# Four buffers for fetched rows in place of eight, from quad 40 on, in a graph network layer

## The chip, the cores and the metric

The kernel runs on one core of a Trainium2 chip. The metric is the time of one execution in microseconds of device time; 1115.52 us is the median of three runs before the change. The core has five engines that run their own instruction streams in order and wait for each other by semaphores: TensorE (PE; its weight loads are listed as PEld), VectorE (DVE), ScalarE (ACT), GpSimd (POOL) and SyncE (SP). DMAs are issued from queues of SP and POOL.

## What is computed

A message-passing layer over 12,500 nodes of 128 features and 400,000 edges that are sorted by destination, with a residual and a layer norm. Cut to what matters:

```python
rbf = exp(-(distances[:, None] - centers) ** 2 / (2 * width * width))     # 50 centers
cut = 0.5 * (cos(pi * distances / 10) + 1) * (distances <= 10)
W = (silu(rbf @ fw1 + fb1) @ fw2 + fb2) * cut[:, None]
messages = (h[src] @ pw + pb) * W
agg = segment_sum(messages, dst, num_segments=12500)
out = layernorm(h + h + silu(agg @ mw1 + mb1) @ mw2 + mb2)
```

Edges longer than 10 contribute nothing, and most edges are longer.

## The kernel before

**Projection.** First all node rows are multiplied by `pw` and stored as a table `proj` in DRAM (lines 562 to 581), so that an edge needs one row of it.

**Packing.** The edges are taken in seven chunks. `pack(c)` (lines 352 to 557) is a generator of many small DVE steps that squeezes out the edges over the cut-off: each of 128 partitions shifts its survivors to the left; POOL then scatters them to a list in DRAM (`packed`, line 451); SP reads the list back (`pair`, line 467), DVE takes it apart (from line 476), PE turns source indices, places and cuts over the partitions, and DVE copies them to `srci`, `dl` and `cut`. Two chunks are in work at a time. Their steps are put between other DVE work by a planner.

**Quads.** What survives is worked on in 141 quads of 4 x 128 edges. For quad q:
- `fetch(q)` (line 593): four indirect DMAs on POOL's queue, 128 rows each, into one buffer `got` of a pool of eight. Quads 0 to 7 are fetched before the table is complete, as raw rows, and projected later (`multiply`).
- `radials`, `basis`, `first`, `tanh`, `silu`, `second`: lengths over SP's queue, ACT's Gaussians, PE, ACT and DVE make the filter `pu` of the quad in PSUM (two buffers).
- `message(q)` (line 671): DVE multiplies `pu` by `got`. It is the last reader of the buffer.
- `place(q)` (line 676): four DVE instructions make one-hot matrices `hot`, scaled by `cut`.
- `sum_up(q)` (line 689): PE multiplies `msg` by `hot`, into a bank shared by two quads.
- `add(q)` (line 712): two quads later DVE adds the result to `aggT` at an offset read from `base_i`.

From step 70 on, nodes whose edges are all in are finished between the quads (`nodes`, line 847); the rest follows the loop.

**The order.** It is written by hand: the loop over q at line 977 issues everything in program order, and each engine runs its part in that order. Within a step come: fetches, `second(q + 1)`, `message(q)`, `sum_up(q)`, `place(q + 1)`, `add(q - 2)`, pieces of packing. A planner with two clocks, `clock` for DVE and `pool` for POOL, decides only where fetches and pieces of packing stand. `fetches(until, most)` (line 343) issues fetches while POOL's clock is not past `until`, up to quad `most`; its cost is 5.15 us for a quad, not before the buffer is free by `summed`. Each step calls it twice, once up to `q + GOT` by the clock, once without regard to the clock up to `q + AHEAD`, which is q+3. At execution the planner's numbers play no part; there POOL runs as far ahead in its own stream as semaphores let it: a fetch waits for the last reader of its buffer, `message(q - 8)`, and for its DMA lane. POOL's stream holds besides the fetches the scatters of line 451 (one a chunk) and, at step 90 or so, the load of a counter `bad_i` (line 1028) that DVE computes after the last chunk.

Of the kernel before, what the change touches and what calls it, by code (L numbers as in the profile page):

```python
# [10 lines left out]
F32 = mybir.dt.float32  # L11
# [8 lines left out]
P = 128  # L20
# [5 lines left out]
QT = 4  # L26
# [12 lines left out]
NQ = QB[-1]  # L39
AHEAD = 3  # L40
AHEAD_X = 4
FROM_X = 8
GOT = 8


CLEARED = 3000
# [10 lines left out]
def kernel(  # L57
# [38 lines left out]
    N, H = x.shape  # L96
# [14 lines left out]
    work = ctx.enter_context(tc.tile_pool(name="work", bufs=2))  # L111
# [61 lines left out]
    def clear(pieces=1, to=N):  # L173

        while pieces and to_clear and to_clear[0][0] < to:
            a, b = to_clear.pop(0)
            nc.scalar.activation(aggT[:, a:b], iota_n[:, :b - a], AF.Copy, scale=0.0)
            pieces -= 1
# [155 lines left out]
    pool = [0.0]  # L334
    there_at = {}
    summed = {}
# [3 lines left out]
    most = [FROM_X]  # L340
    times = [0]

    def fetches(until, most):

        while fetched[0] < min(most, known[0]) and pool[0] <= until:
            q = fetched[0]
            fetch(q, table=x if q < FROM_X else None)
            pool[0] = max(pool[0], summed.get(q - GOT, 0.0)) + 5.15
            there_at[q] = pool[0] + 2.2
            fetched[0] += 1  # L350

# [239 lines left out]
    d_of, rbf_of, ph_of, t_of, s_of, pu_of, got_of, pa_of, hot_of = ({} for _ in range(9))  # L591

    def fetch(q, idx=None, table=None):
        got = work.tile([P, QT, H], F32, name="got", bufs=GOT)
        for j in range(QT):
            i = srci[:, 2 * q + j // 2, j % 2:j % 2 + 1] if idx is None else idx[:, j:j + 1]
            nc.gpsimd.indirect_dma_start(  # L597
                out=got[:, j, :], out_offset=None, in_=proj if table is None else table,
                in_offset=bass.IndirectOffsetOnAxis(ap=i, axis=0))
        got_of[q] = got  # L600
# [14 lines left out]
    def radials(to):  # L615

        while next_o[0] < min(to, -(-NQ // 2)):
            o = next_o[0]
            if not all(chunk_of(q) in stored for q in quads(o)):
                break  # L620
            radial(o, [near_d[2 * q:2 * q + 2].rearrange("(o p) e -> o (p e)", o=1)
                       for q in quads(o)])
            next_o[0] += 1

    def chunk_of(q):
        return max(c for c in range(NC_) if QB[c] <= q)

    def basis(o):
        d, n = d_of.pop(o)
        u = n * 64  # L630
        rbf = work.tile([P, QE], F32, name="rbf")
        nc.scalar.activation(rbf[:u], d[:u], AF.Square, bias=rbf_bias[:u], scale=rbf_scale[:u])  # L632
        nc.scalar.activation(rbf[:u], rbf[:u], AF.Exp, scale=-1.0 / (2.0 * width * width))  # L633
        rbf_of[o] = rbf, n

    def first(o):

        rbf, n = rbf_of.pop(o)
        ph = ps.tile([P, 2, QE], F32, name="ph", bufs=1)
        for h in range(n):  # L640
            p0 = h * 64
            nc.tensor.matmul(ph[:, h, :], w1_sb[p0:p0 + KR], rbf[p0:p0 + KR], start=True, stop=True)  # L642
        ph_of[o] = ph, n

    def tanh(o):
        ph, n = ph_of[o]
        t = work.tile([P, 2, QE], F32, name="t", bufs=1)
        nc.scalar.activation(t[:, :n], ph[:, :n], AF.Tanh, scale=0.5)  # L648
        t_of[o] = t
# [10 lines left out]
    def second(q):  # L660

        s = s_of.pop(q)
        pu = bank("pu")
        nc.tensor.matmul(pu, ones_b[:, :P], bias_b["fb2"].rearrange("k j f -> k (j f)"), start=True,  # L664
                         stop=False)
        for j in range(QT):
            nc.tensor.matmul(pu[:, j * H:(j + 1) * H], s[:, j * P:(j + 1) * P], fw2_h,  # L667
                             start=False, stop=(j == QT - 1))
        pu_of[q] = pu

    def message(q):
        msg = work.tile([P, QT, H], F32, name="msg")
        nc.vector.tensor_mul(msg, pu_of.pop(q).rearrange("p (j f) -> p j f", j=QT), got_of.pop(q))  # L673
        return msg
# [10 lines left out]
    def windows(q):  # L685

        return 1 if chunk_of(q) < WIDE_C else 2

    def sum_up(q, msg):
        hot = hot_of.pop(q)  # L690
        if q % 2 == 0:
            pa_of["two"] = bank("pa").rearrange("p (h n) -> p h n", h=2)
        pa = pa_of[q] = pa_of["two"][:, q % 2, :]
        n = QT // windows(q)
        for j in range(QT):
            k = j // n
            nc.tensor.matmul(pa[:, k * W:(k + 1) * W], msg[:, j, :], hot[:, j, :],  # L697
                             start=(j % n == 0), stop=(j % n == n - 1))
# [3 lines left out]
    def base_of(q, ks=(0, 1)):  # L702
        for k in ks:
            if k == windows(q):
                break
            _, v = nc.values_load_multi_w_load_instructions(
                base_i[0:1, 2 * q + k:2 * q + k + 1], engines=[mybir.EngineType.DVE],
                min_val=0, max_val=N - W,
                skip_runtime_bounds_check_because="bases are destinations, and at most N - W")
            bases[q, k] = v[0]  # L710
# [136 lines left out]
    def nodes(q):  # L847

        if ready:
            normalize(*ready.pop(0))  # L850
        for k, t0 in enumerate(early + last):
            if begin[t0] - 8 == q:
                load_x(t0)
            if begin[t0] + 3 == q and t0 in early:
                if k % 4 == 0:
                    st_of[0] = statistics()
                node_stats(t0, st_of[0][:, k % 4 * 4:])
                if k % 4 == 3 or k + 1 == len(early):
                    scaled(early[k // 4 * 4:k + 1], st_of[0])
            if begin[t0] + 2 == q and t0 in early:  # L860
                node_second(t0, "ms")
            if begin[t0] == q:
                node_first(t0)
            if begin[t0] + 1 == q:
                node_silu(t0)
        if q == NQ - 4:
            for t0 in range(0, NT, 4):
                if t0 not in begin:
                    load_x(t0)
# [26 lines left out]
    def go_on(c):  # L896
        v = next(chunks[c], None)
        if v is None:
            todo.remove(c)
        else:  # L900
            clock[0] += v
# [11 lines left out]
    def multiplies(until):  # L913
        while times[0] < min(FROM_X, fetched[0]) and there_at[times[0]] <= until:
            multiply(times[0])
            times[0] += 1
# [60 lines left out]
    for q in range(NQ):  # L977
        while todo and todo[0] <= chunk_of(min(q + 3, NQ - 1)):
            go_on(todo[0])
        nodes(q)  # L980
        most[0] = min(NQ, q + GOT)
        fetches(clock[0], most[0])
        fetches(math.inf, min(NQ, q + AHEAD + 1))
        assert fetched[0] > min(NQ - 1, q + AHEAD)
        multiplies(max(clock[0], there_at[min(q + 1, NQ - 1)]))
        if q >= CLEAR_Q:
            clear()
        if loads_later and q >= 8:
            nc.sync.dma_start(*loads_later.pop(0))
        radials(q // 2 + 5)  # L990
        if q % 2 == 0:
            if 2 * (q // 2 + 1) < NQ:
                tanh(q // 2 + 1)
        else:
            if q + 3 < NQ:
                first((q + 3) // 2)
            if q + 5 < NQ:
                basis((q + 5) // 2)
        if q + 1 < NQ:
            second(q + 1)  # L1000
        msg = message(q)
        sum_up(q, msg)
        if q > 1:
            base_of(q - 2, (0,))
        if q + 1 < NQ:
            place(q + 1)
        if q > 1:
            base_of(q - 2, (1,))
            add(q - 2)
        if q % 2 == 0 and 2 * (q // 2 + 1) < NQ:  # L1010
            silu(q // 2 + 1)
        clock[0] = max(clock[0], there_at[q])
        summed[q] = clock[0] + 0.7
        clock[0] += (1.9 if q % 2 else 3.1) + 0.3 * (windows(q) - 1)
        if q == 1:
            clear_packed(2, nc.sync)
        if q + 1 < NQ:
            pack_until(max(there_at[q + 1], clock[0] + PACK_US), NC_)
        if NODES - 8 <= q < NODES - 2:
            part_of(*(("mb1", mb1_f) if q < NODES - 5 else ("mb2", mb2_f)), (q - NODES + 8) % 3)  # L1020
        elif q == NODES - 2:
            late["mw2"] = mw2_h = keep.tile([H, H], F32, name="mw2_h")
            nc.vector.tensor_scalar(mw2_h, mw2_sb, 0.5, None, op0=OP.mult)
        if not todo and not counted:
            counted.append(q)
            count()
        elif counted and total is None:
            total = nc.values_load(bad_i[0:1, 0:1], min_val=0, max_val=2 * E)
# [86 lines left out]
```

## Time and profile before

| what | value |
|---|---|
| median of three runs | 1115.52 us (1115.3 to 1117.06) |
| the profiled execution | 1117.06 us, of which the span (first to last instruction) is 1115.3 us |
| mean granted TensorE clock | 0.752 |
| message(0), (36), (97), (140) start at | 122.7, 369.5, 828.5, 1086.3 us |
| fetch(40), (44), (140) start at | 346.7, 370.5, 1047.8 us |

Times within the span count from its first instruction. The four fetches of quad q are the (4q+1)th to (4q+4)th of the 564 instructions of line 597 on POOL, and message(q) is the (q+1)th of the 141 of line 673 on DVE; the timeline lists both. "Idle before" an instruction is time in which its engine had nothing running, with what ended it; "remote" there, and "another core or an unknown queue" in the chain of waits, mean that no releaser was found. Of the chain that ended last, this holds 17%:

```
DVE 24%; PE 22%; another core or an unknown queue 17%; issue 16%; POOL 13%; DMA 3%; ACT 2%; DVEq 2%; SPq 0%; POOLq 0%; ACTq 0%
```

### The profile page before, as it was taken

How to read it: one execution, taken by the hardware profiler on the slowest of the kernel's cores; microseconds unless marked ns; L12 is line 12 of the kernel's file. 1: busy time of each engine (PE TensorE's matmuls, PEld its weight loads, DVE VectorE, ACT ScalarE, POOL GpSimd, SP SyncE). 2: the span in 40 equal slices, each digit the busy share in tenths (PEclk: the TensorE clock that was granted, in tenths of full speed). 3: DMA queues.
4: the chain of work that ended last, by engine and by line, in shares of the span. 5: the costliest groups of instructions: out<-in, count | busy, mean ns of one | idle time of the engine just before them, and what ended most of it. 6: DMA issues, size and time to landing. Idle time of an engine off the chain costs nothing.

```text
span 1115.3 us, 11574 instructions
## 1 busy us (share of the span) xinstructions
PE 648.4 (58%) x3492; PEld 496.0 (44%) x3492; DVE 657.8 (59%) x1857; ACT 297.2 (27%) x473; POOL 560.5 (50%) x585
## 2 busy tenths in 40 slices
PE   6744757654572558526660674276377666666673
PEld 6734545443451446415440453155254554445462
DVE  7902469566583559637980786085364744655594
ACT  5423412113131233102320231042041422241132
POOL 1551366446637555657176416625556655666400
PEclk9867778667687668757785787588587786979796
DMA  7833422222123221313122112232143242142121
GB/s 222 248 100 105 139 72 62 63 69 85 53 71 87 59 57 55 99 40 105 51 82 62 49 46 67 64 107 62 43 121 87 65 126 69 55 125 79 36 61 44
DMA packets 88188, 91.85 MB, mean 82 GB/s; under 512 B 13864, under 2 KB 67832, under 8 KB 88120
## 3 DMA queue, kind: packets, MB, share of 16 engines
q1 hardware_dynamic: 69320, 52.77, 15.6%
q0 software_dynamic: 18544, 38.17, 12.5%
q8 instruction: 29, 0.48, 0.2%
q14 instruction: 39, 0.32, 0.1%
q10 hardware_dynamic: 256, 0.11, 0.0%
HBM read 75.29 MB, written 15.71 MB: 82 GB/s over the span
## 4 chain that ended last, share of the span: by engine, by line
DVE 24%; PE 22%; another core or an unknown queue 17%; issue 16%; POOL 13%; DMA 3%; ACT 2%; DVEq 2%; SPq 0%; POOLq 0%; ACTq 0%
POOL got L597 13%; DVE hot L681 6%; PE pu L667 5%; PE ph L642 5%; DVE s L655 4%; PE pa L697 4%; PE pa L275 2%; DVE msg L673 2%; DVE aggT L716 2%; DMA x<-in_x_dram 1%; PE pu L569 1%; PE pu L664 1%; DMA got<-proj,srci 1%; PE ms L728 1%
## 5 line engine op out<-in xcount | busy, mean ns | idle before, releaser
L597 POOL DMA_INDIRECT got<-proj,srci x532 | 516.6, 971 | 328.1 <-issue 145.3
L697 PE MATMUL pa<-hot,msg 128*128 128x128 f32 x1128 | 193.0, 325 | 194.2 <-DVE msg L673 174.3
L697 PEld LDWEIGHTS pa<-hot,msg 128*128 128x128 f32 x1128 | 173.5, 235 | 207.3 <-DVE msg L673 185.8
L681 DVE TENSOR_SCALAR hot<-iota_n,dl,cut 128x128 f32<-128x128 f32 x564 | 158.4, 352 | 133.9 <-remote 97.5
L673 DVE TENSOR_TENSOR msg<-pu,got 128x512 f32<-128x512 f32 x141 | 96.5, 685 | 183.8 <-remote 132.4
L667 PEld LDWEIGHTS pu<-fw_h,s 128*128 128x128 f32 x1128 | 185.8, 231 | 41.2 <-issue 33.8
L667 PE MATMUL pu<-fw_h,s 128*128 128x128 f32 x1128 | 187.6, 316 | 26.4 <-issue 26.0
L642 PE MATMUL ph<-rbf,w_sb 51*128 51x512 f32 x282 | 113.8, 884 | 145.2 <-DVE s L655 91.0
L648 ACT ACTIVATE t<-ph 128x1024 f32<-128x1024 f32 (+1 forms) x71 | 71.7, 1011 | 280.9 <-remote 151.9
L642 PEld LDWEIGHTS ph<-rbf,w_sb 51*128 51x128 f32 x282 | 29.8, 243 | 166.5 <-issue 124.7
L730 ACT ACTIVATE zt<-ms 128x512 f32<-128x512 f32 (+1 forms) x25 | 14.6, 587 | 324.6 <-remote 124.0
L655 DVE SCALAR_TENSOR_TENSOR s<-t,ph 128x1024 f32<-128x1024 f32 (+1 forms) x71 | 85.8, 1208 | 18.4 <-ACT t L648 12.4
L716 DVE TENSOR_TENSOR aggT<-aggT,pa 128x128 f32 x212 | 60.3, 284 | 13.6 <-remote 5.4
L664 PE MATMUL pu<-fb_b,ones_b 96*128 96x512 bf16 x141 | 64.0, 454 | 0.2 <-issue 0.2
L451 POOL DMA_INDIRECT packed<-line,at_i x7 | 6.9, 992 | 108.8 <-DVE line L447 51.2
L632 ACT ACTIVATE rbf<-d,rbf_bias,rbf_scale 128x512 f32<-128x512 f32 (+1 forms) x71 | 57.1, 804 | 6.8 <-DMA d<-near_d 6.7
L597 POOL DMA_INDIRECT got<-in_x_dram,srci x32 | 32.2, 1007 | 43.2 <-DVE part L519 33.1
L275 PEld LDWEIGHTS pa<-pw_sb,xT 128*128 128x128 f32 (+1 forms) x260 | 40.6, 226 | 27.6 <-ACT xT L571 15.7
L664 PEld LDWEIGHTS <-ones_b 96*128 96x128 bf16 x141 | 14.8, 105 | 82.9 <-issue 82.5
L275 PE MATMUL pa<-pw_sb,xT 128*128 128x128 f32 (+1 forms) x260 | 42.4, 315 | 15.3 <-ACT xT L571 13.0
L633 ACT ACTIVATE rbf<-rbf 128x512 f32<-128x512 f32 (+1 forms) x71 | 44.7, 630 | 2.2
L792 ACT ACTIVATE x<-x,by,rs 128x128 f32<-128x128 f32 x91 | 37.1, 482 | 8.8 <-DVE by L762 8.8
(172 smaller groups left out, 629.1 us busy)
## 6 DMA issues: line engine op xcount, KB each, us to landing
d<-near_d SPq DMA_DIRECT2D x141, 128.0 KB
x<-in_x_dram SPq DMA_DIRECT2D x48, 256.0 KB
got<-proj,srci POOLq DMA_INDIRECT x532
proj<-hp SPq DMA_DIRECT2D x24, 256.0 KB
out_dram<-x SPq DMA_DIRECT2D x24, 256.0 KB
packed<-zero_i SPq DMA_DIRECT2D x6, 188.0 KB
pair<-packed SPq DMA_DIRECT2D x3, 264.0 KB
r_d<-in_edge_weight_dram SPq DMA_DIRECT2D x3, 256.0 KB
```

The source lines that it names most:

```text
L275: nc.tensor.matmul(to[:m, k, :], lT[:, k * P:k * P + m], w, start=False, stop=(k == a + c - 1))
L597: nc.gpsimd.indirect_dma_start(out=got[:, j, :], out_offset=None, in_=proj if table is None else table, in_offset=bass.IndirectOffsetOnAxi ...
L632: nc.scalar.activation(rbf[:u], d[:u], AF.Square, bias=rbf_bias[:u], scale=rbf_scale[:u])
L642: nc.tensor.matmul(ph[:, h, :], w1_sb[p0:p0 + KR], rbf[p0:p0 + KR], start=True, stop=True)
L648: nc.scalar.activation(t[:, :n], ph[:, :n], AF.Tanh, scale=0.5)
L655: nc.vector.scalar_tensor_tensor(s[:, :n], t_of.pop(o)[:, :n], 1.0, ph[:, :n], op0=OP.add, op1=OP.mult)
L664: nc.tensor.matmul(pu, ones_b[:, :P], bias_b["fb2"].rearrange("k j f -> k (j f)"), start=True, stop=False)
L667: nc.tensor.matmul(pu[:, j * H:(j + 1) * H], s[:, j * P:(j + 1) * P], fw2_h, start=False, stop=(j == QT - 1))
L673: nc.vector.tensor_mul(msg, pu_of.pop(q).rearrange("p (j f) -> p j f", j=QT), got_of.pop(q))
L681: nc.vector.tensor_scalar(hot[:, j, :], iota_n[:, :W], dl[:, at[0], at[1]], cut[:, at[0], at[1]], op0=OP.is_equal, op1=OP.mult)
L697: nc.tensor.matmul(pa[:, k * W:(k + 1) * W], msg[:, j, :], hot[:, j, :], start=(j % n == 0), stop=(j % n == n - 1))
L716: nc.vector.tensor_add(to, to, pa[:, k * W:(k + 1) * W])
```

## The change

Fetched rows of quads 0 to 39 go to the eight buffers `got` as before. Those of quads 40 to 140 go to four other buffers, `got_later`. (A negative q, of a fallback branch that does not run with these inputs, goes there too.) The planner's terms follow: a quad of 44 or more is held to have its buffer when quad q-4 is summed, and the bound `most` is q+8 up to quad 44, then q+4.

```diff
+LATER = 40, 4
...
-            pool[0] = max(pool[0], summed.get(q - GOT, 0.0)) + 5.15
+            pool[0] = max(pool[0], summed.get(q - (GOT if q < sum(LATER) else LATER[1]), 0.0)) + 5.15
...
     def fetch(q, idx=None, table=None):
-        got = work.tile([P, QT, H], F32, name="got", bufs=GOT)
+        q_at = q if q >= 0 else NQ
+        got = (work.tile([P, QT, H], F32, name="got", bufs=GOT) if q_at < LATER[0] else
+               work.tile([P, QT, H], F32, name="got_later", bufs=LATER[1]))
...
-        most[0] = min(NQ, q + GOT)
+        most[0] = min(NQ, max(min(q + GOT, sum(LATER)), q + LATER[1]))
```

## The prediction

> **What bounds the kernel now.** I read the page first: its costliest groups, then the waits of the stretch in which the change acts, then the timeline of POOL and DVE, then a table of stretches.
>
> ```profile
> PE 648.4 (58%) x3492; PEld 496.0 (44%) x3492; DVE 657.8 (59%) x1857; ACT 297.2 (27%) x473; POOL 560.5 (50%) x585
> ...
> L597 POOL DMA_INDIRECT got<-proj,srci x532 | 516.6, 971 | 328.1 <-issue 145.3
> ...
> L673 DVE TENSOR_TENSOR msg<-pu,got 128x512 f32<-128x512 f32 x141 | 96.5, 685 | 183.8 <-remote 132.4
> ```
>
> No engine is busy for more than 59% of the span, so the time is in waits. One quad is four fetches on POOL; successive starts lie 1.25 us apart (971 ns each and 0.3 us between them), so a quad takes POOL 5.0 us. Message (line 673) stands behind 183.8 us of DVE's idle time, 132.4 of it with a releaser that the profile cannot name. The waits from 418 us (message of quad 44) to 828.5 us (quad 97), while chunks are still packed, for the most part:
>
> ```profile
> DVE msg L673 <- remote: 58.0, 7, 19.7
> ...
> POOL got L597 <- DVE msg L673: 55.7, 9, 22.3
> DVE hot L681 <- remote: 51.5, 6, 14.0
> POOL packed L451 <- DVE line L447: 51.2, 2, 28.3
> ```
>
> POOL waits for DVE here, and DVE waits for something unnamed. The timeline shows what lies beside the unnamed waits: first POOL, then DVE around 583 us.
>
> ```profile
> 451.97 0.98 POOL L451 DMA_INDIRECT packed<-line,at_i  x1 [14.48 <-DVE first L366]
> ...
> 555.45 0.98 POOL L451 DMA_INDIRECT packed<-line,at_i  x1 [22.88 <-DVE line L447]
> ...
> 673.25 0.98 POOL L451 DMA_INDIRECT packed<-line,at_i  x1 [28.29 <-DVE line L447]
> ...
> 762.47 0.97 POOL L597 DMA_INDIRECT got<-proj,srci  x1 [22.35 <-DVE msg L673]
> ```
> ```profile
> 582.78 0.83 PE L667 MATMUL pu<-fw_h,s 128*128 128x128 f32 x6
> ...
> 598.96 0.69 DVE L673 TENSOR_TENSOR msg<-pu,got 128x512 f32<-128x512 f32 x1 [17.41 <-remote]
> ...
> 613.67 1.12 DVE L681 TENSOR_SCALAR hot<-iota_n,dl,cut 128x128 f32<-128x128 f32 x4 [14.01 <-remote]
> ```
>
> The reader is to see a cycle. POOL runs ahead until its queue comes to an entry that needs DVE at a certain quad (the scatter of line 451, and at 762 us the load of bad_i, line 1028); it waits there for 14 to 28 us while DVE uses up the rows already fetched; then eight buffers are free and it issues fetches without a pause. From 555.4 to 608.6 us it issues 41 in a row. In this burst PE's last matmuls end at 583.6, but message starts only at 598.96; it waits for PE's semaphore, whose next recorded update is at 598.9. The update after it comes at 613.6, with the matmuls it reports over by 601.8. So while POOL issues for long, PE's completions arrive late, and DVE, ACT and then PE stand still. I don't know the cause; the coincidence holds for all DVE gaps of over 9 us after 418 us (14.0, 10.9, 17.4, 14.0, 19.7, 9.8, 16.1: 102 us), which lie in the four bursts of 28 to 41. By stretches (us, then PE, PEld, DVE, ACT and POOL busy with counts, granted clock, DMA share, GB/s):
>
> ```profile
> 467.60:498.40 30.80, 6.40 (x21) 4.25 (x21) 5.73 (x13) 0.00 (x0) 19.27 (x21) 0.50 0.16 46
> ...
> 577.00:617.60 40.60, 8.04 (x38) 6.29 (x39) 8.72 (x25) 2.84 (x4) 23.94 (x26) 0.58 0.25 71
> 617.60:684.30 66.70, 48.55 (x274) 35.70 (x270) 55.77 (x166) 16.73 (x22) 23.93 (x25) 0.86 0.20 57
> 684.30:728.90 44.60, 8.48 (x29) 6.03 (x29) 9.18 (x23) 8.46 (x17) 26.42 (x28) 0.50 0.20 58
> ...
> 828.50:1073.60 245.10, 165.44 (x892) 124.43 (x893) 145.26 (x430) 69.88 (x120) 136.47 (x144) 0.81 0.29 83
> ```
>
> **The change part by part.** It moves no instruction. Stepping through the planner's numbers (lines 343 to 350 and 981 to 984): its POOL clock stands later than its DVE clock from quad 33 on, so from step 40 on exactly q+4 quads are issued at step q, by line 983 alone, and the new term `summed[q - 4]` is always below the POOL clock it is compared with. The new bound on `most` is that same q+4. So the order on every engine stays, and the scatters stay where they are. What changes is one wait: fetch(q) for q of 44 and up waits for message(q-4) in place of message(q-8). Quads 40 to 43 go to fresh buffers; their old wait was long over (fetch 40 started at 346.7, message 32 at 325.7): nothing.
>
> *The wait that goes.* At its three scatters and its load of bad_i POOL now has less to wait for: the entry before scatter 4, 5 and 6 is fetch(q+3), which itself waits for message(q-1), one step ahead of the scatter. So 14.5 + 22.9 + 28.3 + 22.4 = 88 us of POOL waiting are spread over single quads, and no burst can find more than four free buffers: 20 us of issue where it was 35 to 53.
>
> *The wait that comes* is message(q-4). Queued behind it on POOL is the scatter, and behind that the pair load on SP (line 467), for which DVE waits at line 476. POOL can be three quads behind, 15 us; the planner leaves 16 us (at scatter 4 its POOL clock is 322.1 and its DVE clock 310.3, and it adds 4.0), so I put this at nothing, 5 us for each of three if that cover is gone. Rows come early enough: a fetch started at 885.40 had landed by 887.7, so the last row of a quad is there 6 us after its first fetch, and four quads at the fastest POOL pace are 20 us.
>
> *The new pace.* The trace has stretches in which POOL already stands against its buffers, each pause ending 0.3 us after message(q-8), no scatter wait among them. There eight buffers act as four would: POOL is at its limit either way. From the fetch starts: quads 8 to 16 51.9 us, 33 to 36 16.4, 44 to 54 62.2, 63 to 68 28.5, 79 to 82 20.2, 91 to 93 17.5, 101 to 140 245.3. Sum 442.0 us for 70 quads: **6.31 us a quad**, from 5.47 to 6.72 but for two quads at 8.75. A bit of the longest:
>
> ```profile
> 885.40 0.94 POOL L597 DMA_INDIRECT got<-proj,srci  x1 [3.19 <-DVE msg L673]
> ...
> 907.82 1.05 POOL L597 DMA_INDIRECT got<-proj,srci  x1 [7.75 <-DVE msg L673]
> ...
> 925.86 0.94 POOL L597 DMA_INDIRECT got<-proj,srci  x1 [3.26 <-DVE msg L673]
> ```
>
> Twelve fetches (three quads, 14.7 us) go between one pause and the next.
>
> *The sum.* Message 36 stays at 369.5. POOL then waits for message 40; with POOL idle a quad takes 5.2 us (messages 63 to 68, 544.8 to 570.7, POOL idle from 532.6 to 555.4), so message 40 comes at 390.3 (was 394.7) and fetch 44 at 390.6. Fetch 140 follows 96 x 6.31 = 606 us later, at 996.4 (was 1047.8). It starts 0.3 us after message 136, so that one is at 996.1 (was 1068.6); the last four messages take 17.7 us as now, and 29.0 us follow to the end of the span: 1042.8. With the 1.8 us around the span (1117.06 against 1115.3) 1044.6; the profiled execution is 1.5 us above the median of 1115.52, so **1043**. The gain of 72 us is mostly the stalls of 102 us, less what lockstep costs between them.
>
> DVE isn't a new bound: between 418 and 828.5 us it is busy for 247 us in 53 quads, 4.7 us a quad.
>
> **A rule against it.** Fetches are now issued some 40 us ahead of their message (fetch 101 ended at 807.2, message 101 started at 850.7). The Trainium skill, "DMA: Bandwidth & Descriptors", "Rules for kernel authors", says to issue a DMA early and wait for it late; by that rule alone a halved lead gains nothing and only the end of the loop would tell. The other rule is from "SBUF — State Buffer", "Who interferes with whom": "PE and ACT never wait on anyone." By it POOL's bursts are harmless and the time would stay at about 1116. The row of 577 to 617.6 us, with ACT busy for 2.84 us and PE for 8.04 of 40.6 while POOL issues, doesn't look like that, and I go by the row.
>
> **The rivals.** *Conserved (0.13).* PE's late completions may belong to each microsecond of POOL's work and not to long bursts. From message 44 to 136 92 quads take 650.5 us, POOL works for 92 x 5.0 = 460 of them; at 5.2 us a quad in the other 190.5 us (36.6 quads) the work leaves 55.4 quads, 8.3 us each. In lockstep 5.0 us of work then bring 0.60 of a quad and 2.07 us more are needed: 7.07 us, 96 x 7.07 = 679, the end at 1116 to 1118 and the median near 1116. For it: the stalls start within bursts of three quads too (5.4 us before 924.9). Against: lockstep was measured at 6.31.
>
> *Slower (0.15).* With four buffers the pauses come more often. In the last stretch 39 quads take 245.3 us, 195 of them work, so 50 us are pauses, 3.9 for each of 13 bursts of three. If the shorter lead cuts the bursts to 1.5 quads, a quad costs 5.0 + 3.9/1.5 = 7.6 us: 96 x 7.6 = 730, the time 1167. It decides from below 1.9 quads to a burst. For it: only one quad of slack is left beyond a burst of three. Against: the rows for the next three messages are in SBUF when the burst ends, and after 395 us message never waits for landed rows.
>
> *No change of order or wait at all* I leave out: 24 pauses after 395 us end on message.
>
> **How the numbers follow.** The forecast has 0.72. Its own range is the pace from 5.47 to 6.72 us: 96 x 5.47 = 525 gives 962, 96 x 6.72 = 645 gives 1082, and 15 us more if the scatters' cover goes, 1097. The lowest pace comes from three quads alone, so I cut it at 975 (5.6 us). Up to 1105 some of the conserved case is taken in (6.95 us, two quads to a burst). Left out are most of the other two and the lowest tail, some 2 in 10. A measurement of this kernel tells 0.2% (2.2 us) from no change. Faster: 0.72 and half of the conserved case, 0.78. Within 0.2%: 0.04. Slower: 0.15 and 0.03 of the conserved case, 0.18.
>
> **What would show it.** Right: from 390 us on POOL's bursts hold 16 fetches at most, the waits of line 451 fall from 51 us (line 447) to a few, DVE's gaps of over 9 us go, fetches start 0.3 us after message(q-4), and message 97 comes near 750 us (was 828.5). Wrong: message waiting for landed rows (DMA got), pauses after every one or two quads, DVE waiting at line 476 for its pair, or gaps as long as before in short bursts.

## The result and the profile after

The changed kernel takes 1057.59 us (median of four runs), 0.947 of the time before, with an interval from 0.940 to 0.954. In two later groups of runs, on two different chips, it took 0.945 (0.940 to 0.950) and 0.939 (0.930 to 0.949). Ratios leave out disturbed executions, which the medians in microseconds include, so the two can differ by some thousandths. The profiled execution has a span of 1055.7 us. The lines of its page that answer to those of before are these (engines' busy time, the chain that ended last, and the groups of fetches and messages; message has two lines now, one for each pool of buffers):

```profile
PE 655.7 (62%) x3492; PEld 495.9 (47%) x3492; DVE 657.5 (62%) x1857; ACT 297.5 (28%) x473; POOL 562.0 (53%) x585
...
DVE 31%; PE 28%; another core or an unknown queue 21%; issue 11%; POOL 2%; ACT 2%; DMA 2%; DVEq 2%; SPq 0%; ACTq 0%; POOLq 0%
...
L600 POOL DMA_INDIRECT got_later<-proj,srci x404 | 390.8, 967 | 263.2 <-DVE msg L676 139.3
...
L676 DVE TENSOR_TENSOR msg<-pu,got_later 128x512 f32<-128x512 f32 x101 | 69.1, 684 | 65.1 <-remote 34.7
...
L676 DVE TENSOR_TENSOR msg<-pu,got 128x512 f32<-128x512 f32 x40 | 27.3, 684 | 57.9 <-remote 50.0
```

No engine works less: POOL, DVE and ACT are busy as long as before, and the instruction order of PE, DVE, ACT and SP is the same. What fell is waiting: 123 us of DVE's idle time stand behind message (65.1 and 57.9) where it was 183.8. POOL left the chain that ended last (13% before, 2% now), while the chain's share without a named releaser is 21% now and was 17%. The timeline of POOL shows the pauses, in brackets with what ended them:

```profile
389.00 1.06 POOL L600 DMA_INDIRECT got_later<-proj,srci  x1 [21.47 <-DVE msg L676]
...
416.13 0.94 POOL L600 DMA_INDIRECT got_later<-proj,srci  x1 [6.99 <-DVE msg L676]
...
474.95 0.94 POOL L600 DMA_INDIRECT got_later<-proj,srci  x1 [6.30 <-DVE msg L676]
...
640.55 0.98 POOL L452 DMA_INDIRECT packed<-line,at_i  x1 [4.29 <-DVE line L448]
```

The one long pause is the change of buffers, as POOL waits for message 40. The three scatters from 450 us on, before which POOL stood for 14.5, 22.9 and 28.3 us, now have 4.3 us before them at most, and the 22.4 us at the load of bad_i are gone. The longest run of fetches without a pause after it is 20, where POOL issued 41 DMAs in a row (a scatter and 40 fetches). The waits from message 44 to message 97 (us in total, times, longest):

```profile
POOL got_later L600 <- DVE msg L676: 55.0, 14, 7.0
...
DVE hot L684 <- remote: 30.4, 5, 9.0
...
DVE msg L676 <- remote: 14.6, 5, 4.6
```

In the same 53 quads message and hot waited 109.5 us (58.0 and 51.5) for something unnamed before; it is 45 now, the longest 9.0 in place of 19.7. The semaphore records tell what these waits end on. From 400 us on, DVE has 20 waits of over 3 us, 161.9 us in all, in the profile of before that end on an update of PE's semaphore over 2 us after the last matmul that makes such an update had ended; now it has 18, 105.0 us in all. The difference of 57 us is nearly the whole gain of the span (59.6 us). No wait of over 3 us from 400 us on ends so late on an update of DVE's or ACT's. Below, "late waits" are waits of DVE counted in this way.

This stretch and the one to message 136 (columns as in the table of before):

```profile
415.20:755.30 340.10, 219.44 (x1148) 161.89 (x1149) 246.60 (x682) 93.53 (x142) 211.72 (x215) 0.78 0.29 82
755.30:1001.90 246.60, 166.28 (x869) 122.15 (x867) 141.03 (x417) 70.79 (x120) 145.92 (x154) 0.78 0.30 82
```

The first took 410.5 us before, with the same 247 us of DVE work in it: it saves 70.4 us, more than the whole. The second, 240.1 us before, takes 246.6 for 39 quads and gives 6.5 back; the last four messages, 17.7 us before, take 24.2 and give back as much; the head gains 3.

### The profile page after: what moved, and what is told of

Same layout as the page of the kernel before. It is cut to its first block, busy times and chain, and to the rows that moved or that the text cites. A ratio compares the mean times of both kernels' runs of the same rounds, so it can differ in the third digit from the quotient of the medians.

```text
span 1055.7 us, 11583 instructions
## 1 busy us (share of the span) xinstructions
PE 655.7 (62%) x3492; PEld 495.9 (47%) x3492; DVE 657.5 (62%) x1857; ACT 297.5 (28%) x473; POOL 562.0 (53%) x585
## 4 chain that ended last, share of the span: by engine, by line
DVE 31%; PE 28%; another core or an unknown queue 21%; issue 11%; POOL 2%; ACT 2%; DMA 2%; DVEq 2%; SPq 0%; ACTq 0%; POOLq 0%
DVE hot L684 8%; PE pu L670 6%; PE ph L645 5%; PE pa L700 5%; DVE s L658 4%; DVE msg L676 3%; PE pa L276 3%; PE ms L731 2%; DVE aggT L719 2%; PE pu L667 2%; DVE r_d L428 2%; POOL got_later L600 1%; DVEq L709 1%; DVE nodes L419 1%
## 5 line engine op out<-in xcount | busy, mean ns | idle before, releaser
L600 POOL DMA_INDIRECT got_later<-proj,srci x404 | 390.8, 967 | 263.2 <-DVE msg L676 139.3
L700 PE MATMUL pa<-hot,msg 128*128 128x128 f32 x1128 | 188.4, 319 | 138.5 <-DVE msg L676 120.0
L700 PEld LDWEIGHTS pa<-hot,msg 128*128 128x128 f32 x1128 | 168.7, 229 | 151.8 <-DVE msg L676 132.9
L670 PEld LDWEIGHTS pu<-fw_h,s 128*128 128x128 f32 x1128 | 191.8, 238 | 36.5 <-issue 28.4
L670 PE MATMUL pu<-fw_h,s 128*128 128x128 f32 x1128 | 192.8, 322 | 22.3 <-issue 22.1
L600 POOL DMA_INDIRECT got<-proj,srci x128 | 126.7, 990 | 85.2 <-issue 38.0
L676 DVE TENSOR_TENSOR msg<-pu,got_later 128x512 f32<-128x512 f32 x101 | 69.1, 684 | 65.1 <-remote 34.7
L658 DVE SCALAR_TENSOR_TENSOR s<-t,ph 128x1024 f32<-128x1024 f32 (+1 forms) x71 | 85.8, 1208 | 16.1 <-ACT t L651 8.1
L719 DVE TENSOR_TENSOR aggT<-aggT,pa 128x128 f32 x212 | 60.4, 285 | 14.5 <-issue 6.0
L667 PE MATMUL pu<-fb_b,ones_b 96*128 96x512 bf16 x141 | 65.7, 466 | 0.6 <-issue 0.6
L676 DVE TENSOR_TENSOR msg<-pu,got 128x512 f32<-128x512 f32 x40 | 27.3, 684 | 57.9 <-remote 50.0
L276 PE MATMUL pa<-pw_sb,xT 128*128 128x128 f32 (+1 forms) x260 | 42.7, 317 | 22.1 <-ACT xT L572 18.9
```

What stands on the lines that cost most here:

```text
L276: nc.tensor.matmul(to[:m, k, :], lT[:, k * P:k * P + m], w, start=False, stop=(k == a + c - 1))
L600: nc.gpsimd.indirect_dma_start(out=got[:, j, :], out_offset=None, in_=proj if table is None else table, in_offset=bass.IndirectOffsetOnAxi ...
L658: nc.vector.scalar_tensor_tensor(s[:, :n], t_of.pop(o)[:, :n], 1.0, ph[:, :n], op0=OP.add, op1=OP.mult)
L719: nc.vector.tensor_add(to, to, pa[:, k * W:(k + 1) * W])
```

## The experiments

Lockstep stands below for a POOL that waits for a free buffer every few quads. Theory A is that of the prediction: POOL comes early to a queue entry that needs DVE, then issues into eight free buffers without a pause, and in such a burst PE's completions come late. Theory B: the number of buffers, or the long lead of the rows, makes the stalls. Theory C: each microsecond of POOL's work costs the same wherever it lies. The kernels of the next four runs shared a chip, on which the kernel before took 1133.04 us. In every experiment PE, DVE, ACT and SP keep the order of before; only POOL's stream differs.

**The queue's order alone, with eight buffers.**

```diff
+        while q >= 45 and issued[0] < min(NQ, q + 8, known[0]):
+            fetch(issued[0])
+            issued[0] += 1
```

The planner's arithmetic is as before; the fetches up to q+7 simply stand ahead of a scatter.

> Eight buffers as before, every other engine's order as before; from step 45 on POOL's stream holds the fetches up to quad q+7 ahead of a scatter, and not only those up to q+3. Theory A (POOL waits at a queue entry that comes too early for the rows it may still fetch; then eight free buffers give one long burst of issue, in which PE's completions come late): the scatter waits of 14 to 28 us shrink to under 5, bursts hold some 12 to 20 fetches, DVE's gaps of over 9 us after 460 us go, time 1050 to 1075, although the rows are still some 40 us ahead. Theory B (the number of buffers or the long lead itself makes the stalls): 1105 to 1120, gaps as before. Theory C (each microsecond of POOL's work costs the same wherever it lies): 1110 to 1120.

Measured: 1076.71 us, 0.946 of before (0.932 to 0.959). The median lies 2 us above the span of microseconds expected, on a chip on which before takes 17 us more; the ratio is the one of the change. Its waits from 400 us on:

```profile
DVE hot L685 <- remote: 76.1, 11, 9.5
...
DVE msg L677 <- remote: 22.8, 8, 7.8
...
POOL packed L455 <- DVE line L451: 3.5, 1, 3.5
```

The long scatter waits are gone, and no unnamed wait is over 9.5 us (19.7 before; under 9 was expected), with all eight buffers in use and rows there 45.7 us ahead of their message (from the end of a quad's fetches, mean of quads 48 to 136; 42.5 before, 18.9 in the changed kernel). Theory B falls: the gain comes with eight buffers and the long lead as well. C falls too, as POOL does the same work. The late waits are 17, 112.8 us in all.

**Pauses alone.** Ten memsets behind every third quad's fetches, in the kernel before.

```diff
         got_of[q] = got
+        if q >= 44 and q % 3 == 2:
+            for _ in range(10):
+                nc.gpsimd.memset(idle, 0)
```

> The kernel before with ten small memsets on POOL (some 4.6 us) after every third quad's fetches from quad 44 on: 33 pauses in the issue of DMAs, 150 us of added POOL work, buffers and waits as before. Theory A: PE's late completions come through in each pause, the gaps of 10 to 20 us in the four long bursts shrink to under 9 us, and where POOL stood at its buffers anyway the memsets take the place of the pauses: 1060 to 1100, faster than before although POOL does more. Theory B: gaps as before, 1115 to 1150. Theory C: added POOL work is at best free: 1115 to 1170.

Measured: 1077.91 us, 0.952 (0.942 to 0.962): 155 us of added POOL work (33 pauses of 4.7 us) and yet 5% faster. The unnamed waits of message and hot end at 9.7 us and not at 19.7 (I expected under 9). The late waits fall to 16, 96.3 us in all. This is the cleanest sign that the burst, not POOL's load, costs the time. The slower POOL also shortens the lead to 9.8 us, but the run before this one gains as much with 45.7.

**Four buffers from quad 8 on.**

```diff
-LATER = 40, 4
+LATER = 8, 4
```

(Here, too, the planner's numbers are kept as in before, and only the issue is held to q+3.)

> As after, but four buffers from quad 8 on and not from 40; all other engines' order as before. Theory A: the long bursts of after at 170 to 202, 250 to 291 and 331 to 367 us break up, with DVE's gaps of 6.6, 10.5, 10.5 and 22.6 us in them: 20 to 35 us below after, 1022 to 1038. Theory B: the same or a little lower. Theory C, and the theory that after's gain came from something that begins at quad 40 alone: 1053 to 1062.

Measured: 1065.2 us, 0.945 (0.936 to 0.954): nothing that can be told from the change. The 20 to 35 us below the changed kernel that theory A expected did not come. The early part does gain: message 36 starts at 346.9 us and not at 370.8. But from message 36 to 97 a quad takes 6.55 us (6.30 in the changed kernel), and the last four messages 28.4 us. Why the early gain is given back isn't settled; the changed kernel was not on this chip, so part of it may be the chip's.

**Three buffers from quad 40 on.**

```diff
-LATER = 40, 4
+LATER = 40, 3
```

(The planner's numbers are kept as in before, and the issue is held to q+2.)

> As after, but three buffers from quad 40 on and a quad's fetch placed two steps ahead. Theory A: a pause comes after three quads at most anyway, so the pace stays near 6.4 us a quad as long as DVE never waits for landed rows: 1050 to 1075. The theory that a short lead cuts the bursts (the slower rival of the prediction): below two quads a pause, 7.0 us a quad or more, message waiting for landed rows: 1100 to 1170.

Measured: 1073.23 us, 0.950 (0.940 to 0.961). From 400 us on:

```profile
DVE hot L689 <- remote: 71.2, 10, 9.2
...
DVE msg L681 <- remote: 22.6, 6, 5.5
...
DVE msg L681 <- DMA got_later<-proj,srci: 7.6, 4, 3.4
```

Now message does wait for landed rows, but for 7.6 us in all. The slower rival of the prediction doesn't come true even with a buffer less.

The next four shared another chip (before 1119.03 us). The changed kernel itself was among them:

> The changed kernel itself, beside the next three on one chip. All theories: 0.947 of the time before.

Measured: 1057.55 us, 0.945 (0.940 to 0.950).

**What sets the pace in lockstep.** Two kernels add memsets of 0.47 us to the changed kernel behind each quad's fetches, five in the first (the diff) and one in the second.

```diff
         got_of[q] = got
+        if q >= 44:
+            for _ in range(5):
+                nc.gpsimd.memset(idle, 0)
```

> After, with five memsets (2.35 us) behind each quad's fetches from quad 44 on: POOL needs 7.35 us a quad. If such a pause lets PE's completions through (A1, and A2 at its lower end), nothing else is lost: 7.4 us a quad, 96 quads, some 95 us more than after, 1150, and no DVE gap of over 6 us that ends on PE. If lockstep is POOL's work plus pauses that come on top (6.41 + 2.35 = 8.76): 1280.

Measured: 1150.26 us, 1.029 (1.020 to 1.037). The two longest items of message's waits from 400 us on:

```profile
DVE msg L680 <- DMA got_later<-proj,srci: 252.2, 75, 6.7
...
DVE msg L680 <- PE pu L674: 18.0, 6, 4.0
```

POOL now issues almost without a wait of its own (from 400 us on three of over 1 us, the longest 2.9; 7.5 us a quad, 7.35 of it work), message waits for rows, and the unnamed waits of message and hot are gone, with no late wait left. So most of the 1.4 us a quad that the changed kernel takes above POOL's 5.0 is not POOL's: its late waits alone are 105.0 us, 1.1 us for each of 96 quads. A pause of 2.3 us after each quad buys them off, at a price above their worth.

> After, with one memset of 0.47 us on POOL behind each quad's fetches from quad 44 on (46 us of added POOL work). Theory A1 (any break in the issue of fetches lets PE's completions through): DVE's gaps of over 6 us go, pace 5.6 to 6.0 us a quad, 1005 to 1035. Theory A2 (only a pause of some 2 to 4 us does, until the last fetch has landed): gaps as in after, 1055 to 1100.

Measured: 1037.1 us, 0.925 (0.919 to 0.930), faster than the changed kernel beside it. From 400 us on:

```profile
DVE msg L680 <- remote: 48.9, 14, 6.6
...
DVE hot L688 <- remote: 25.4, 7, 5.8
```

The outcome lies between the two expectations: a break of 0.47 us after each quad shortens the unnamed waits (6.6 at most, from 9.0; 13 late waits, 65.7 us in all) and lowers the pace to 6.23 us, but does not end them.

**Eight buffers, the order mended from step 8 on.**

```diff
+        while q >= 8 and issued[0] < min(NQ, q + 8, known[0]):
```

> Eight buffers throughout, the fetches up to q+7 put ahead of the scatters from step 8 on (where the chunk is known), all other engines' order as before. Theory A: the early bursts break up as with four buffers from quad 8 on (some 20 us), and the last quads run with POOL done (6 us): 1025 to 1045, below after. Theory B (fewer buffers are what helps): 1060 to 1085, above after.

Measured: 1039.52 us, 0.929 (0.925 to 0.933), 18 us below the changed kernel. Message 36 starts at 355.4 us (370.8 in the first profile of the changed kernel), and the last four messages take 17.8 us (24.2 there). These two stretches hold some 22 us, more than the 18. The first belongs to quads that the change leaves alone, so this run doesn't show that eight buffers in mended order are better from quad 40 on; mended from step 45 on they gave 0.946, the ratio of the change.

**Three runs on a chip that behaves otherwise.** The next group came to a chip on which the kernel before takes 828.18 us. The first run puts one long row of memsets into the kernel before.

```diff
     def fetch(q, idx=None, table=None):
+        if q == 62:
+            for _ in range(88):
+                nc.gpsimd.memset(idle, 0)
         got = work.tile([P, QT, H], F32, name="got", bufs=GOT)
```

> The kernel before, with 88 memsets (41 us) on POOL ahead of the fetches of quad 62, when eight quads' rows are there: POOL is busy for 41 us but issues no DMA. Theory A (the issue of fetches makes PE's completions late): from some 3 us after the last fetch ahead of the memsets to their end no DVE gap of over 6 us, 5 to 5.5 us a quad; then a burst of eight quads with gaps of over 9 us. Rival (any long work of POOL does it): gaps of 10 us and more within the memsets too.

Measured: 867.61 us (one run; 39 us more than before there). Groups of its page, then the timelines of POOL and DVE at the memsets:

```profile
L601 POOL DMA_INDIRECT got<-proj,srci x532 | 520.5, 978 | 178.3 <-issue 141.4
...
L677 DVE TENSOR_TENSOR msg<-pu,got 128x512 f32<-128x512 f32 x141 | 96.4, 684 | 123.3 <-DMA got<-proj,srci 105.2
...
L685 DVE TENSOR_SCALAR hot<-iota_n,dl,cut 128x128 f32<-128x128 f32 x564 | 158.3, 357 | 4.7 <-PE pa L701 4.3
```
```profile
389.24 41.47 POOL L597 MEMSET idle<- 128x376 int32 x88
```
```profile
437.36 0.69 DVE L677 TENSOR_TENSOR msg<-pu,got 128x512 f32<-128x512 f32 x1 [39.65 <-DMA got<-proj,srci]
```

POOL issues 215 and then 318 DMAs without a pause and PE's completions are in time: the whole trace has no late wait, nor has that of either of the two runs below. Hot, which stood 133.9 us idle before, waits 4.7. POOL bounds the kernel there, message waits for rows, POOL never gets ahead, and so eight quads were not in store when the memsets began; DVE stood through them. Whether a POOL that is long busy without issuing DMAs delays PE is therefore not shown by this run. The memsets of the other runs speak against it for short stretches: in the run with five a quad POOL was busy almost throughout and the unnamed waits were gone.

The other two add breaks to the kernel in mended order (from step 8 on): one memset of 0.47 us after each quad, and a very short one after each of a quad's four DMAs.

```diff
         got_of[q] = got
+        if q >= 8:
+            nc.gpsimd.memset(idle, 0)
```

> Eight buffers with the fetches up to q+7 ahead of the scatters from step 8 on, and one memset of 0.47 us behind each quad's fetches from quad 8 on. If the two gains (18 and 20 us below after, beside each other on one chip) add: 0.908 to 0.92 of before, 1015 to 1028 where before is 1119. If both break the same bursts: 0.925 to 0.933, 1035 to 1044.

Measured: 870.96 us against 828.18, 1.051 (1.047 to 1.054).

```diff
+            if q >= 8:
+                nc.gpsimd.memset(idle[:, :16], 0)
```

> The same with a memset of 16 columns (some 0.1 us) behind each single fetch in place of one of 376 columns behind each quad. If the number of breaks counts: at or below the one with a longer break a quad, 0.90 to 0.92 of before. If a break must have some length: no better than without breaks, 0.925 to 0.945.

Measured: 841.51 us, 1.017 (1.015 to 1.019). Neither expectation could be tested, as there was nothing to break. POOL bounds there: from quad 101 to quad 140 it takes 5.30 and 5.07 us a quad in these two and 5.01 in the run with the long row of memsets, which over 133 quads makes 39 and 9 us; the times are 43 and 13 us above before. The mended order without breaks was not run on that chip, nor these two where PE's completions come late. The last run is the changed kernel once more.

> The changed kernel once more, on whatever chip comes. Where PE's completions come late while POOL issues (before near 1120): 0.945 of before, 1055 to 1062. Where they do not (before near 828, POOL without a pause, message waiting for rows): the change takes lead from a kernel that POOL bounds, and can gain nothing: 0.995 to 1.03 of before, 824 to 853.

Measured: 1053.29 us, 0.939 (0.930 to 0.949), on a chip with late completions. What the change does where they are in time was therefore not measured.

## Why the prediction held, and where it was off

The forecast was 1043, the measured median 1057.59; the gain was 59 us where 73 were forecast (72 and 60 in the spans).

- *No instruction moves, one wait changes.* Right: the order of the four other engines is the same, and from 416 us on 29 of POOL's 32 pauses of over 1 us before a fetch end 0.3 us after message(q-4), the others up to 1.7 us after it.
- *The scatter waits and the long bursts go.* Right: of 65.7 us of waits before the scatters from 450 us on 4.6 are left, and the 22.4 at the load of bad_i went; bursts of at most 20 fetches (I had said 16; messages free buffers while POOL issues). One DVE gap of 9.0 us is left where seven of over 9 made 102. One of these seven, the 16.1 us before message 93, was no late completion: its matmuls themselves came late, one each 2.1 us with nothing named that they wait for, and the last ended 0.3 us before the message.

```profile
796.57 0.37 PE L667 MATMUL pu<-fw_h,s 128*128 128x128 f32 x1 [1.73 <-issue]
798.67 0.37 PE L667 MATMUL pu<-fw_h,s 128*128 128x128 f32 x1 [1.73 <-issue]
...
801.49 0.69 DVE L673 TENSOR_TENSOR msg<-pu,got 128x512 f32<-128x512 f32 x1 [16.13 <-PE pu L667]
```

So beside a burst PE can also be slow to start its matmuls, and not only to report them.

- *The pace.* 6.31 us a quad was taken from stretches of the trace in which POOL stood against eight buffers. Measured: 615.8 us from fetch 44 to fetch 140, **6.41**, ten us too few in 96 quads. This is the larger mis-sized term. The three runs of the changed kernel have 6.41, 6.45 and 6.39 us, and eight buffers in mended order 6.38 and 6.59: at their limit eight act about like four, as was assumed.
- *The tail.* "The last four messages take 17.7 us as now": measured 24.2, the other mis-sized term, 6.5 us. Before, POOL had ended its last fetch at 1052.5 us, 16 us ahead of message 136; now it ends at 1009.5, 8 us after it (1001.9), so the last messages run beside a POOL that still issues; that this lengthens them was not tested by itself. With eight buffers in mended order it is 17.8 again, in both runs.
- *The head.* Message 40 at 388.1 (forecast 390.3), fetch 44 at 389.0 (390.6): right. The 5.2 us a quad behind it were said to be those of an idle POOL, but POOL was idle only up to 555.4 of the stretch from 544.8 to 570.7; messages 61 to 65, 534.9 to 555.1, give 5.05, which would have made it 389.7. The other differences are under 3 us: message 36 starts 1.3 us later, fetch 140 starts 2.9 us after message 136 and not 0.3, and the part behind message 140 takes 29.7 us and not 29.0.
- *Conserved* fell with the runs of the pauses and of the mended order; *slower* fell with three buffers. The wait that comes, message(q-4), cost DVE nothing at line 476's place: no wait for a pair shows among its waits. That a measurement tells 0.2% from no change was too hopeful: on one chip before took from 1108.06 to 1131.16 us.
- *The rules of the skill.* The Trainium skill, "DMA: Bandwidth & Descriptors", "Rules for kernel authors", has DMAs issued early. The change shortens the lead from 42.5 to 18.9 us and gains; but with a lead of 45.7 us and the order mended from step 45 on the ratio is the same, so the early issue was not what hurt. "SBUF — State Buffer", "Who interferes with whom", says that PE never waits on anyone; on the chips of before and after, PE's reports were late beside POOL's issue, on one chip they were not. The rule speaks of SBUF ports, and no run here shows that these are the place.

What stays open is the cause of the late completions. The runs show when they come (all 38 late waits in the profiles of before and after begin 5.8 us or more after POOL's last pause of over 0.4 us), what lets them through (a pause in POOL's issue: 0.47 us after each quad left 13 late waits, 2.35 us none) and that one chip had none. A property of the kernel alone it is not. Whether the issue by POOL or the transfers that it starts hold PE up was not told apart, as each pause held back both.

Another rival was not tested: the recording. Each execution here has a recorded span and granted clock. On the chips with late completions records are missing: of the 1132 updates that DVE makes, 805 are recorded in before, 772 in after and 881 in the run with five memsets; in the run with the long row of memsets, on the other chip, 1122 are. In before 114 of 115 are recorded from 1053 us on, when POOL has ended its last fetch. So where PE is late, the recording falls short as well. One may cause the other, or both may have one cause; whether the kernel has these waits when nothing is recorded, no run shows.

## What to carry to other kernels

A queue entry that waits for a late event should stand behind everything that could run ahead of it; if it stands early, the engine idles in front of it and then works off its backlog in one burst, beside which others may stall. Fewer buffers break up the burst, and so does mending the order, which keeps the lead as well (0.947 and 0.946 for the quads from 40 or so on). When idle time has no releaser, look at what another engine does without a pause beside it, and try a short pause there before looking for a missing buffer. Look too at whether the trace has all its records at that place.

## What was not expected of the hardware

The kernel before took 1116 to 1133 us in the measurement at the start and on three chips, and 828 us on another, with the same instructions; an indirect DMA takes POOL as long there (978 ns in the run with one row of memsets, 971 ns before). What differs in the records is PE's completions (29 late waits of DVE, 230.1 us, in the whole profile of before and none in that run) and how many updates were recorded at all. A gain won on one chip against such waits, like breaks in POOL's issue (0.925, with four buffers and one break a quad), can be a loss on another (1.051, with eight buffers in mended order and one break a quad). These are two kernels; neither was run on both kinds of chip.
